# Where a mixture-of-experts result gets its weight: ScalarE after the fetch, or GpSimd before the scatter

## The chip, the core and the metric

The kernel runs on one core of a Trainium2 chip, in one launch. The metric is the device time of one execution in microseconds (us). Below, PE is TensorE, DVE is VectorE, ACT is ScalarE, POOL is GpSimd and SP is SyncE, which only issues DMAs.

## The reference

Two transformer-like layers work on x of 8 x 256 tokens of width 128. Layer 0 adds a small state-space block and a ternary feed-forward net. Layer 1 adds a "test-time training" attention (a state W per head, updated chunk by chunk) and a mixture of experts. Only the last part is touched by the change:

```python
scores = sigmoid(xf @ gate_w.T + gate_b)               # 2048 tokens, 8 experts
top_scores, top_idx = top_k(scores, 2)
top_scores = top_scores / (top_scores.sum(-1, keepdims=True) + 1e-06)
hdn = gelu(einsum('th,ehf->etf', xf, w1) + b1[:, None, :])
y = einsum('etf,efh->eth', hdn, w2) + b2[:, None, :]
routed = einsum('te,eth->th', comb, y)                 # comb: the two weights, 0 elsewhere
shared = (gelu(xf @ sw1 + sb1) @ sw2 + sb2) * 0.1
x = x + attention + routed + shared
```

So each token has two expert results, each is multiplied by one number, the token's normalised score for that choice, and both are added to the token's residual.

## The kernel before, in words

Everything is float32. Tokens lie in chunks n = 0 to 3 of 64 positions, with 4 pairs of batch rows each: a chunk is a tile of 128 partitions x 4 pairs x 128 features (`x1[n]`), and a pair is one of 16 "units" u of the attention.

**Order of the work.** After layer 0 the main loop (L1297) runs through the units. One turn works on three of them at once: unit u+1 makes its keys, unit u its normalised states, unit u-1 its gradient and its update of W, and unit u-2 its output. Between these steps `filler()` puts in steps of other work: the end of layer 0's feed-forward net, the routing (turn 5), the shared expert, and from turn 6 to turn 14 the routed expert tiles. In the loop the orders of DVE and SP are the program's own (`manual_schedule`, L1291). The orders of PE, ACT and POOL are made by a list scheduler from priorities and estimated times. For the last units, from L1413 on, the orders of PE and ACT too are written by hand; POOL's never is.

**Routing.** `norm()` (L327) makes a row of ROW = 130 numbers for each token: 128 normalised features, the token's number (column D) and the rank of its first choice's expert (column D+1). `choose(0)` and `choose(1)` (L365) take the best and second score of each token into `wgt`, and `find_slots()` (L387), in a later step, gives each of the two choices a place in an HBM array `xg_dram`, sorted by expert. `scatter()` (L254) then writes rows there with indirect DMAs from POOL, 32 in all. `weights()` (L758) normalises the scores of all tokens at turn 9 with four DVE instructions.

**Routed tiles.** 39 tiles (NJ) of 128 rows follow, three to a group (GJ). For each: SP loads the expert's weights and the rows (L815, L824), PE transposes the rows (L831), makes the hidden layer (L855), ACT applies gelu (L860), PE makes the result (L870), DVE adds the bias into `ysum` (L881). `places()` (L834) works out on DVE, with two instructions for a group, where in `y_dram` each row of the result goes; it is put off to a quiet place in DVE's order. `scatter_results()` (L885) writes the 128 rows of a tile's result there with an indirect DMA from POOL. These are queued in `ready`, and `transfers(k)` in the main loop issues up to k of them at three places of a turn.

**The turn of a transfer.** Each indirect DMA has an ordering edge to the POOL instruction last noted in `turn` (L162). It is noted by `rsqrt()` (L171), which makes an inverse deviation by a multiply-add (L174) and a power of -1/2 (L175) on POOL, and by `normalise()` (L1112, L1113), which makes the start of the gradient on POOL. So a transfer does not come ahead of the POOL work that the program has just issued.

**The end.** When all tiles are scattered, `get(8)` (L1435) fetches the results again, eight tiles (first and second choice of 4 chunks). `weigh()` (L936) multiplies each with four ACT instructions, one for a pair of batch rows, at hand-chosen places (`weigh(1)`, `weigh(1)`, `weigh(4)`, `weigh(1)`, `weigh(1)`), and `add()` (L943) adds it to `x1[n]`: three on POOL (`put(3, z.last)`, L1462) and five on DVE. Then `x1` is stored.

Of the kernel before, what the change touches and what calls it, by code (L numbers as in the profile page):

```python
# [26 lines left out]
NBP = B // 2  # L27
# [4 lines left out]
NT = NCH * NBP  # L32
# [3 lines left out]
GJ = 3  # L36
# [5 lines left out]
NXG = E * CAP + (NJ - 2 * B * S // P) * P  # L42


ROW = D + 2

SLOTS = (4, 1, 2, 0, 5, 3)
SLOTS_2 = (5, 2, 4, 5, 3, 1)
# [3 lines left out]


EARLY, ROUTE = 6, 5
NORMAL = 9
AT_SILU, AT_SILU_1, AT_XP = 7, 10, 11
FFN = ((0, 2), (1, 11), (2, 16), (3, 3), (4, 4))
SHARED = ((4, 2), (5, 6), (14, 3), (15, 3), (16, 2))
# [20 lines left out]
def tile_two_layers(ctx: ExitStack, tc: tile.TileContext, t: dict, out: bass.AP):  # L79
    nc = tc.nc  # L80

    const = ctx.enter_context(tc.tile_pool(name="const", bufs=1))
    small = ctx.enter_context(tc.tile_pool(name="small", bufs=2))
# [3 lines left out]
    side = {}  # L87
# [72 lines left out]
    turn = []  # L160

    def transfer(**what):  # L162
        ins = nc.gpsimd.indirect_dma_start(**what).ins  # L163
        tc.add_manual_dep(
            ins, turn[0].name,
            mybir.DependencyInfo(mybir.DependencyClass.NoSync, mybir.DependencyReason.DATA),
            reason="in turn",
        )
        return ins
# [10 lines left out]
    def later(f):  # L180
        pending.append(f)
# [49 lines left out]
    def empty_rows(pool):  # L231
        rows = pool.tile([P, ROW], F32, tag="empty", name="empty", bufs=1)
        nc.gpsimd.memset(rows, 0.0)
        nc.gpsimd.memset(rows[:, D : D + 1], float(2 * B * S))
        nc.gpsimd.memset(rows[:, D + 1 : ROW], -1.0)
        return rows

    slot = resident_i("slot", [P, NT, 2])
# [6 lines left out]
    wgt = resident("wgt", [P, NT, 2])  # L245
# [20 lines left out]
    def ffn_steps(n):  # L266

        s = {}
# [94 lines left out]
        mine = slice(n * NBP, (n + 1) * NBP)  # L363

        def choose(k):  # L365

            shape = [P, NBP, E]
            left = t_e(s["w"][2]) if k else s["s"]
            m = wgt[:, mine, k]
            nc.vector.tensor_reduce(m, left, AX.X, ALU.max)  # L370
            eq = t_e(s["w"][k])
            nc.vector.tensor_tensor(eq, left, m.unsqueeze(2).to_broadcast(shape), ALU.is_equal)
            nc.vector.tensor_tensor(eq, eq, rank[:, None, :].to_broadcast(shape), ALU.mult)
            mr = small.tile([P, NBP], F32, tag="tk_mr", name="tk_mr") if k else s["row"][:, :, D + 1]
            nc.vector.tensor_reduce(mr, eq, AX.X, ALU.max)
            nc.vector.tensor_tensor(eq, eq, mr.unsqueeze(2).to_broadcast(shape), ALU.is_equal)
            if k == 0:
                nc.vector.scalar_tensor_tensor(t_e(s["w"][2]), eq, -4.0, s["s"], ALU.mult, ALU.add)
            else:
                sel = s["w"][3]  # L380
                nc.vector.tensor_tensor(sel, s["w"][0], s["w"][1], ALU.add)
                s["pn"] = bank("pn")[:, : 2 * NBP * E].rearrange("p (a c) -> p a c", a=2)
                nc.tensor.matmul(s["pn"][:, 0, :], lhsT=all_ones, rhs=sel, start=True, stop=True)
                nc.tensor.matmul(s["pn"][:, 1, :], lhsT=earlier, rhs=sel, start=True, stop=True)
                later(find_slots)

        def find_slots():  # L387

# [300 lines left out]
    def routing_steps():  # L689
# [65 lines left out]
            )  # L755
            load_first_tiles()

        def weights():  # L758
            tot = small.tile([P, NT], F32, tag="tk_tot", name="tk_tot")
            nc.vector.tensor_tensor(tot, wgt[:, :, 0], wgt[:, :, 1], ALU.add)  # L760
            nc.vector.tensor_scalar(tot, tot, 1e-6, None, ALU.add)
            nc.vector.reciprocal(tot, tot)
            nc.vector.tensor_tensor(wgt, wgt, tot.unsqueeze(2).to_broadcast([P, NT, 2]), ALU.mult)

        return constants, [tiles, rows], [results], weights

    def shared_steps(n, half):

# [37 lines left out]


    known, scattered = [], []
    ew, xg, xgT, hidden, ysum, unsummed, ats = {}, {}, {}, {}, {}, [], {}

    def expert_weights(j):
        if j < NJ:
# [13 lines left out]
    def routed_tokens_T(g):  # L826
        if g < NG:
            pt = bank("pxg")[:, : GJ * P].rearrange("p (j q) -> p j q", j=GJ)
            src = xg.pop(g)
            for j in range(GJ):  # L830
                nc.tensor.transpose(pt[:, j, :], src[:, j, 0:D], ident)  # L831
            ats[g] = side["moe"].tile([P, GJ], I32, tag="ats", name="ats", bufs=3)

            def places():  # L834

                first = small.tile([P, GJ], F32, tag="first", name="first")
                nc.vector.tensor_tensor(
                    first, src[:, :, D + 1], tile_rank[:, g * GJ : (g + 1) * GJ], ALU.is_equal
                )
                nc.vector.scalar_tensor_tensor(  # L840
                    ats[g], first, -float(B * S), src[:, :, D], ALU.mult, ALU.add
                )
                known.append(g)

            quiet.append(places)
            xgT[g] = side["moe"].tile([P, GJ, P], F32, tag="xgT", name="xgT")
            nc.scalar.copy(xgT[g], pt)
# [37 lines left out]
    def scatter_results(g, i):  # L885
        assert g in known
        scattered.append(g * GJ + i)
        ins = transfer(
            out=y_dram, out_offset=bass.IndirectOffsetOnAxis(ap=ats[g][:, i : i + 1], axis=0),
            in_=ysum[g][:, i, :], in_offset=None, bounds_check=2 * B * S - 1, oob_is_err=False,  # L890
        )

        tc.declare_no_dep(ins, group="results", reason="distinct rows")
        tc.add_to_no_dep_group("results", ins)
# [23 lines left out]
    def result_steps(n, k):  # L918

        held = {}  # L920

        def fetch():

            if n == NCH - 2:
                y = wk[:, k * NBP * D : (k + 1) * NBP * D]
            elif n < NCH - 1:
                y = side["moe"].tile([P, NEW], F32, tag="ew", name="yc", bufs=4)[:, 0 : NBP * D]
            else:
                y = side["moe"].tile([P, NBP * D], F32, tag="rhid", name="yc")
            held["y"] = y.rearrange("p (b d) -> p b d", b=NBP)  # L930
            row = k * B * S + n * TB
            nc.sync.dma_start(
                out=held["y"], in_=y_dram[row : row + TB, :].rearrange("(b p) d -> p b d", p=P)
            )

        def weigh():  # L936
            for bp in range(NBP):
                nc.scalar.activation(
                    held["y"][:, bp, :], held["y"][:, bp, :], AF.Copy,
                    scale=wgt[:, n * NBP + bp, k : k + 1],  # L940
                )

        def add(behind=None):  # L943
            if behind is None:
                nc.vector.tensor_tensor(x1[n], x1[n], held["y"], ALU.add)  # L945
# [8 lines left out]
        return fetch, weigh, add  # L954


    Wst = [l1.tile([P, 2, HH, HD], F32, tag=f"W_{bp}", name=f"W_{bp}") for bp in range(NBP)]
# [318 lines left out]
    constants, to_tiles, to_loads, weights = routing_steps()  # L1276
# [7 lines left out]
    fill[NORMAL] += [weights]  # L1284
# [12 lines left out]
    for u in range(units - 1):  # L1297
# [3 lines left out]
        z, g, o = live.get(u), live.get(u - 1), live.pop(u - 2, None)  # L1301
# [74 lines left out]
            g.outputs_std()  # L1376
        transfers(2)
        for _ in range(gets.get(u, 0)):
            fetch, weigh, add = results.pop(0)
            fetch()  # L1380
            weigh()
# [4 lines left out]
    weighed, added = [], []  # L1386

    def last_filler(u, k):

# [3 lines left out]
    def get(k):  # L1393
        assert NJ - 1 in scattered and not ready
        for _ in range(min(k, len(results))):
            fetch, weigh, add = results.pop(0)
            fetch()
            weighed.append(weigh)
            added.append(add)

    def weigh(k):
        for _ in range(min(k, len(weighed))):
            weighed.pop(0)()

    def put(k, behind=None):
        for _ in range(min(k, len(added))):
# [3 lines left out]
    results = [results[k] for k in (0, 1, 2, 3, 6, 7, 4, 5)]  # L1410
# [22 lines left out]
    g.steps_of_W()  # L1433
    transfers(len(ready))
    get(8)  # L1435
    weigh(1)
    o.outputs_T()
    flush()
    g.outputs()
    z.open_queries()  # L1440
    weigh(1)
    o.open_mix()
    o.mix_heads()
    last_filler(u, len(fill[u]))
    u += 1
    z.means(first)
    g.outputs_std()
    weigh(4)
    z.gradient(first)
    last_filler(u, 2)  # L1450
    z.steps_of_W(first)
# [10 lines left out]
    put(3, z.last)  # L1462
    z.outputs(HALVES)
    z.last_std()
    weigh(1)
    last_filler(u, len(fill[u]))
    z.normalise_outputs(first)
    z.outputs_T(first)
# [2 lines left out]
    put(1)  # L1471
    g.residual()
    flush_all()
    weigh(1)
    put(2)
    z.open_mix()
    z.mix_heads(first)
# [109 lines left out]
```

## Time and profile before

| what | value |
|---|---|
| median of 4 runs | 579.21 us (573.93 to 580.35) |
| the profiled execution's own time | 574.86 us |
| its span in the profile | 573.2 us |
| granted TensorE clock over the span | 0.988 |
| PE busy | 534.1 us (93%) |
| DVE busy | 404.7 us (71%) |
| POOL busy | 296.3 us (52%) |
| ACT busy | 259.2 us (45%) |
| turns with routed tiles, about 305 to 530 us | PE has little idle time |
| last units, 530 to 573 us | PE busy 30.2 us of 43, DVE 35.5, ACT 29.2, POOL 24.5 |

The span is what the profile shows from the first to the last instruction; the time has 1.7 us more around it. A line of a timeline gives the start, the duration (of a run of equal instructions), the engine, the kernel's line, the operation, the tiles it writes and reads, how often, and in brackets the idle time of that engine just before it with what ended it.

### The profile page before, as it was taken

The page shows a single profiled execution, that of the slowest core. Times are in us where ns is not written, and L with a number is a line of the kernel's source. Part 1 is how long each engine was busy: PE and PEld are TensorE (multiplying, and loading weights), DVE is VectorE, ACT ScalarE, POOL GpSimd, SP SyncE. Part 2 cuts the span into 40 slices and gives each one's busy share as a digit, 9 for nine tenths or more (in the row PEclk, how much of TensorE's full clock was granted, in tenths as well). Part 3 has the DMA queues.
Part 4 walks back from the last instruction along what each step waited for, and adds up shares of the span by engine and source line. Part 5 has one row for each costly group of instructions (what it writes and reads, how often), then busy time and mean ns, then how long its engine had stood idle before and what let it go on. Part 6 is the DMA issues. An engine that isn't in the chain of part 4 may idle for free. (4 is left out here: it accounts for less than half of the span.)

```text
span 573.2 us, 14199 instructions
## 1 busy us (share of the span) xinstructions
PE 534.1 (93%) x5891; PEld 369.3 (64%) x5891; DVE 404.7 (71%) x649; ACT 259.2 (45%) x472; POOL 296.3 (52%) x258
## 2 busy tenths in 40 slices
PE   6999999999999999999979999999999999999695
PEld 3443655465456546476766887877787777878584
DVE  4697353457931476667979788869789777757995
ACT  4655545315430542224416363452645454453685
POOL 5216103851680156443674557565865737384861
PEclk9999999999999999999989999999999999989989
DMA  7900200000000000000153434442443433300312
GB/s 274 396 39 26 61 2 6 33 1 3 9 26 4 1 9 15 17 0 2 43 182 98 146 112 149 148 150 97 159 150 103 150 111 134 99 15 4 99 51 74
DMA packets 25200, 45.89 MB, mean 80 GB/s; under 512 B 3875, under 2 KB 16297, under 8 KB 24624
## 3 DMA queue, kind: packets, MB, share of 16 engines
q1 hardware_dynamic: 22864, 40.75, 21.6%
q0 software_dynamic: 2272, 4.24, 2.3%
q8 instruction: 46, 0.75, 0.5%
q14 instruction: 18, 0.15, 0.1%
HBM read 38.30 MB, written 7.13 MB: 79 GB/s over the span
## 5 line engine op out<-in xcount | busy, mean ns | idle before, releaser
L293 PE MATMUL pm<-g,h 128*128 128x512 f32 x256 | 113.6, 594 | 0.0
L175 POOL TENSOR_TENSOR rstd<-rs_v,neg_half 128x16 f32<-128x16 f32 x31 | 93.1, 3003 | 2.6
L293 PEld LDWEIGHTS pm<-g,h 128*128 128x128 f32 x256 | 48.2, 190 | 59.8 <-issue 57.3
L1112 POOL TENSOR_TENSOR gx<-xh,gam 128x1024 f32<-128x1024 f32 (+1 forms) x17 | 37.9, 2229 | 72.2 <-DVE er L1111 60.1
L860 ACT ACTIVATE rhid<-phd,ew 128x128 f32<-128x128 f32 x156 | 44.5, 374 | 41.1 <-issue 21.0
L297 ACT ACTIVATE g<-pm,cols 128x512 f32<-128x512 f32 x32 | 22.0, 687 | 75.5 <-PE pm L293 75.5
L174 POOL TENSOR_SCALAR rs_v<-var 128x16 f32<-128x16 f32 x31 | 7.3, 235 | 91.2 <-DVE var L1048 90.5
L163 POOL DMA_INDIRECT y_dram<-ys,ats x39 | 43.2, 1107 | 8.9 <-issue 8.5
L1048 DVE TENSOR_REDUCE var<-sq 128x16 f32<-128x1024 f32 (+1 forms) x33 | 38.9, 1180 | 9.4 <-ACT sq L1042 9.4
L855 PE MATMUL phd<-xgT,ew 128*128 128x128 f32 x312 | 43.5, 280 | 1.1 <-DMA ew<-in_moe_w 1.0
L855 PEld LDWEIGHTS phd<-xgT,ew 128*128 128x128 f32 x312 | 39.3, 191 | 7.5 <-issue 5.5
L1042 ACT ACTIVATE sq<-o 128x1024 f32<-128x1024 f32 (+1 forms) x17 | 17.1, 1010 | 54.7 <-DVE o L1031 54.7
L870 PE MATMUL pyr<-ew,rhid 128*128 128x128 f32 x312 | 41.4, 276 | 0.0
L163 POOL DMA_INDIRECT xg_dram<-xn,slot x32 | 35.9, 1121 | 8.6 <-issue 7.7
L1113 POOL TENSOR_TENSOR gx<-gx,u 128x1024 f32<-128x1024 f32 (+1 forms) x17 | 38.7, 2276 | 1.3
L870 PEld LDWEIGHTS pyr<-ew,rhid 128*128 128x128 f32 x312 | 38.0, 192 | 0.7 <-issue 0.5
L1088 DVE TENSOR_TENSOR u<-rows_b,pv 128x1024 f32<-128x1024 f32 x16 | 19.5, 1217 | 23.9 <-PE pv L976 23.9
L1260 PE MATMUL po<-wo,oT 128*128 128x128 f32 x256 | 33.1, 285 | 0.7 <-ACT oT L993 0.7
L1260 PEld LDWEIGHTS po<-wo,oT 128*128 128x128 f32 x256 | 31.9, 202 | 1.2 <-ACT oT L993 0.9
L976 PE MATMUL pk<-wk,xnT 128*128 128x512 f32 x64 | 32.2, 623 | 0.2 <-DVE o L1031 0.2
L976 PE MATMUL pv<-wv,xnT 128*128 128x512 f32 x64 | 31.4, 613 | 0.0
L1005 PE MATMUL pq<-xnT,wq 128*128 128x256 f32 x128 | 30.8, 383 | 0.7 <-DVE B L1207 0.7
(233 smaller groups left out, 1067.5 us busy)
## 6 DMA issues: line engine op xcount, KB each, us to landing
ew<-in_moe_w SPq DMA_DIRECT2D x39, 578.0 KB
xg<-xg_dram SPq DMA_DIRECT2D x39, 65.0 KB
h<-in_h SPq DMA_DIRECT2D x2, 1024.0 KB
yc<-y_dram SPq DMA_DIRECT2D x6, 256.0 KB
rows_g<-in_rows_g SPq DMA_DIRECT2D x1, 1024.0 KB
rows_b<-in_rows_b SPq DMA_DIRECT2D x1, 1024.0 KB
w<-in_w SPq DMA_DIRECT2D x3, 256.0 KB
x<-in_x SPq DMA_DIRECT2D x3, 256.0 KB
```

What stands on the lines that cost most here:

```text
L163: ins = nc.gpsimd.indirect_dma_start(**what).ins
L175: turn[:] = [nc.gpsimd.tensor_tensor(dst, v[:, :width], neg_half[:, :width], ALU.pow).ins]
L293: nc.tensor.matmul(pm, lhsT=w[:, k, m * P : (m + 1) * P], rhs=s[src][:, k, :], start=(k == 0), stop=(k == 3),)
L855: nc.tensor.matmul(ph[:, ms], lhsT=w[:, ms], rhs=xgT[j // GJ][:, j % GJ, :], start=True, stop=True)
L860: nc.scalar.activation(hid[:, m, :], ph[:, ms], AF.Gelu, bias=w[:, C_EB1 + m : C_EB1 + m + 1])
L870: nc.tensor.matmul(py, lhsT=hid[:, m, :], rhs=w[:, C_EW2 + m * D : C_EW2 + (m + 1) * D], start=(m == 0), stop=(m == 3),)
L976: nc.tensor.matmul(pp[:, j, :], lhsT=xT, rhs=w[:, j * 512 : (j + 1) * 512], start=True, stop=True)
L1005: nc.tensor.matmul(pq[:, i, :], lhsT=wq[:, (h0 + i) * P : (h0 + i + 1) * P], rhs=xnT[n][:, 2 * half : 2 * half + 2, :], start=True, stop=True,
L1048: nc.vector.tensor_reduce(v[:, heads], sq[:, heads], AX.X, ALU.add)
L1112: nc.gpsimd.tensor_tensor(g, xh, gam2[:, k], ALU.mult)
L1113: turn[:] = [nc.gpsimd.tensor_tensor(g, g, self.t[:, k], ALU.add).ins]
L1260: nc.tensor.matmul(self.po, lhsT=self.oT[:, hp, :], rhs=wo[:, hp, :], start=False, stop=(hp == HH - 1),)
```

## The change

The row of a token grows from 130 to 132 numbers. The normalisation of the scores moves from turn 9 into `choose(1)`, chunk by chunk, behind the issue of its two matmuls, and writes into the row: column D+2 gets the first weight less the second, column D+3 the second. `places()` works out, with two more DVE instructions for a group, the weight of each row's choice (`gains`): the difference times "this tile is the first choice's expert", plus the second. `scatter_results()` multiplies the tile's result in place by that number on POOL, ahead of the indirect DMA, and notes that multiply in `turn`. `weigh()` and all its calls go, so that the fetched tiles are added as they come.

```diff
-ROW = D + 2
+ROW = D + 4
...
-NORMAL = 9
...
-        nc.gpsimd.memset(rows[:, D + 1 : ROW], -1.0)
+        nc.gpsimd.memset(rows[:, D + 1 : D + 2], -1.0)
...
                 nc.tensor.matmul(s["pn"][:, 1, :], lhsT=earlier, rhs=sel, start=True, stop=True)
+                weights()
                 later(find_slots)
+
+        def weights():
+
+            w = wgt[:, mine, :]
+            tot = small.tile([P, NBP], F32, tag="tk_tot", name="tk_tot")
+            nc.vector.tensor_tensor(tot, w[:, :, 0], w[:, :, 1], ALU.add)
+            nc.vector.tensor_scalar(tot, tot, 1e-6, None, ALU.add)
+            nc.vector.reciprocal(tot, tot)
+            nc.vector.tensor_tensor(
+                s["row"][:, :, D + 2 : ROW], w, tot.unsqueeze(2).to_broadcast([P, NBP, 2]), ALU.mult
+            )
+            one, two = s["row"][:, :, D + 2], s["row"][:, :, D + 3]
+            nc.vector.tensor_tensor(one, one, two, ALU.subtract)
...
-        def weights():
-            tot = small.tile([P, NT], F32, tag="tk_tot", name="tk_tot")
-            nc.vector.tensor_tensor(tot, wgt[:, :, 0], wgt[:, :, 1], ALU.add)
-            nc.vector.tensor_scalar(tot, tot, 1e-6, None, ALU.add)
-            nc.vector.reciprocal(tot, tot)
-            nc.vector.tensor_tensor(wgt, wgt, tot.unsqueeze(2).to_broadcast([P, NT, 2]), ALU.mult)
...
+            gains[g] = side["moe"].tile([P, GJ], F32, tag="gains", name="gains", bufs=3)
...
                 nc.vector.scalar_tensor_tensor(
                     ats[g], first, -float(B * S), src[:, :, D], ALU.mult, ALU.add
                 )
+                nc.vector.tensor_tensor(first, first, src[:, :, D + 2], ALU.mult)
+                nc.vector.tensor_tensor(gains[g], first, src[:, :, D + 3], ALU.add)
...
         scattered.append(g * GJ + i)
+        y = ysum[g][:, i, :]
+        turn[:] = [nc.gpsimd.tensor_scalar(y, y, gains[g][:, i : i + 1], None, ALU.mult).ins]
         ins = transfer(
...
-        def weigh():
-            for bp in range(NBP):
-                nc.scalar.activation(
-                    held["y"][:, bp, :], held["y"][:, bp, :], AF.Copy,
-                    scale=wgt[:, n * NBP + bp, k : k + 1],
-                )
-
...
     get(8)
-    weigh(1)
     o.outputs_T()
     flush()
     g.outputs()
     z.open_queries()
-    weigh(1)
...
     g.outputs_std()
-    weigh(4)
     z.gradient(first)
...
     z.last_std()
-    weigh(1)
...
     flush_all()
-    weigh(1)
     put(2)
```

More of the change, by code (lines that the diff above doesn't have):

```diff
@@ L756, in results @@
             load_first_tiles()
-        def weights():
-            tot = small.tile([P, NT], F32, tag="tk_tot", name="tk_tot")
-            nc.vector.tensor_tensor(tot, wgt[:, :, 0], wgt[:, :, 1], ALU.add)
-            nc.vector.tensor_scalar(tot, tot, 1e-6, None, ALU.add)
-            nc.vector.reciprocal(tot, tot)
-            nc.vector.tensor_tensor(wgt, wgt, tot.unsqueeze(2).to_broadcast([P, NT, 2]), ALU.mult)
-        return constants, [tiles, rows], [results], weights
+        return constants, [tiles, rows], [results]
     def shared_steps(n, half):
@@ L808, in tile_two_layers @@
     known, scattered = [], []
-    ew, xg, xgT, hidden, ysum, unsummed, ats = {}, {}, {}, {}, {}, [], {}
+    ew, xg, xgT, hidden, ysum, unsummed, ats, gains = {}, {}, {}, {}, {}, [], {}, {}
     def expert_weights(j):
@@ L952, in add @@
                 )
-        return fetch, weigh, add
+        return fetch, add
     Wst = [l1.tile([P, 2, HH, HD], F32, tag=f"W_{bp}", name=f"W_{bp}") for bp in range(NBP)]
@@ L1275, in tile_two_layers @@
         fill[turn_u] += [steps.pop(0) for _ in range(k)]
-    constants, to_tiles, to_loads, weights = routing_steps()
+    constants, to_tiles, to_loads = routing_steps()
     fill[ROUTE - 1] += [open_moe]
@@ L1283, in tile_two_layers @@
     fill[ROUTE] += to_loads
-    fill[NORMAL] += [weights]
     routed = [lambda j=j: routed_step(j) for j in range(NJ + 1)]
@@ L1378, in tile_two_layers @@
         for _ in range(gets.get(u, 0)):
-            fetch, weigh, add = results.pop(0)
+            fetch, add = results.pop(0)
             fetch()
-            weigh()
             fetched.append(add)
@@ L1385, in tile_two_layers @@
     first, second = HALVES
-    weighed, added = [], []
+    added = []
     def last_filler(u, k):
@@ L1395, in get @@
         for _ in range(min(k, len(results))):
-            fetch, weigh, add = results.pop(0)
+            fetch, add = results.pop(0)
             fetch()
-            weighed.append(weigh)
             added.append(add)
-    def weigh(k):
-        for _ in range(min(k, len(weighed))):
-            weighed.pop(0)()
     def put(k, behind=None):
```

## The prediction, made before the changed kernel ran

> **What bounds the kernel now.** I read the page's busy times first, then busy time by stretch, then the groups by shape for the lines the change touches, then the timelines of the last 45 us and of one routed turn. The page and the stretches:
>
> ```profile
> PE 534.1 (93%) x5891; PEld 369.3 (64%) x5891; DVE 404.7 (71%) x649; ACT 259.2 (45%) x472; POOL 296.3 (52%) x258
> ```
> ```profile
> 285.00:530.00 245.00, 231.34 (x3551) 187.97 (x3549) 195.14 (x259) 111.23 (x240) 151.14 (x98) 0.99 0.37 118
> 530.00:573.00 43.00, 30.16 (x438) 26.02 (x428) 35.50 (x51) 29.24 (x84) 24.48 (x16) 0.92 0.25 75
> ```
>
> In the columns of the second fence (length, PE, weight loads, DVE, ACT, POOL) PE is busy 231 of the 245 us from 285 to 530: it sets the pace there, and POOL and DVE have about 94 and 50 us free. In the last 43 us no engine is full: there a chain through DVE, PE, ACT and POOL decides. What the change removes and the only sort of POOL work near to what it adds:
>
> ```profile
> L938 ACT ACTIVATE yc<-yc,wgt 128x128 f32<-128x128 f32 x24 | 7.2, 389 | 0.0
> L938 ACT ACTIVATE wk<-wk,wgt 128x128 f32<-128x128 f32 x8 | 2.5, 390 | 0.0
> ```
> ```profile
> L163 POOL DMA_INDIRECT y_dram<-ys,ats x39 | 43.2, 1107 | 8.9 <-issue 8.5
> L174 POOL TENSOR_SCALAR rs_v<-var 128x16 f32<-128x16 f32 x31 | 7.3, 235 | 91.2 <-DVE var L1048 90.5 <-issue 0.2
> L619 POOL COPY bpad<-headT 128x1024 f32<-128x1024 f32 x1 | 1.5, 1494 | 0.0
> ```
>
> The timeline of the end, ACT, then POOL, then DVE:
>
> ```profile
> 547.40 5.95 ACT L938 ACTIVATE yc<-yc,wgt 128x128 f32<-128x128 f32 x20
> 553.83 1.64 ACT L784 ACTIVATE hid<-pm,shared_w 128x256 f32<-128x256 f32 x4 [0.48 <-PE pm L778]
> ...
> 563.87 1.26 ACT L938 ACTIVATE wk<-wk,wgt 128x128 f32<-128x128 f32 x4
> 565.68 1.13 ACT L993 COPY oT<-poT 128x512 f32<-128x512 f32 x2 [0.55 <-PE poT L989]
> 566.71 1.28 ACT L938 ACTIVATE wk<-wk,wgt 128x128 f32<-128x128 f32 x4
> ```
> ```profile
> 531.68 2.91 POOL L175 TENSOR_TENSOR rstd<-rs_v,neg_half 128x16 f32<-128x16 f32 x1
> 534.77 1.06 POOL L163 DMA_INDIRECT y_dram<-ys,ats  x1 [0.18 <-issue]
> 536.13 0.97 POOL L163 DMA_INDIRECT y_dram<-ys,ats  x1 [0.30 <-issue]
> 537.17 0.67 POOL L174 TENSOR_SCALAR rs_v<-var 128x16 f32<-128x16 f32 x1
> 537.93 3.91 POOL L175 TENSOR_TENSOR rstd<-rs_v,neg_half 128x16 f32<-128x16 f32 x1
> ```
> ```profile
> 541.87 0.69 DVE L1107 TENSOR_TENSOR xh<-xh,rstd 128x512 f32<-128x512 f32 x1 [0.24 <-POOL rstd L175]
> ...
> 566.41 1.42 DVE L945 TENSOR_TENSOR x<-x,yc 128x512 f32<-128x512 f32 x2
> 567.75 1.47 DVE L945 TENSOR_TENSOR x<-x,wk 128x512 f32<-128x512 f32 x2
> ```
>
> The reader is to see that after each block of weighting ACT still waits for PE (0.48 and 0.55 us): ACT was early, not late. And that the last two scatters stand ahead of a POOL power that DVE waits for.
>
> **The weighting goes from ACT.** 32 instructions of 0.39 us, 12.4 us with their gaps, all between 543.0 and 568.0. The first block (543.01 to 544.28) is followed by a copy that waits 1.26 us for PE; the five blocks from 547.40 by 0.48 us of waiting for PE; the one at 563.87 by 0.55 us; the last ends at 567.99, before DVE's last add, which starts at 568.52 directly behind the add ahead of it. The consumers do not wait either: POOL's three adds start at 557.83 and are tied to DVE's last gradient step at 557.7, and DVE's five adds from 565.50 run back to back, in an order that does not change. I take a gain of 0. The bound below is 0.5 us, in case the order of the last microseconds loosens a little.
>
> **The multiply on POOL.** 39 of 128x128 with a number per partition; no row of the trace is such an instruction. The nearest in kind is L174, 0.20 us undisturbed for 16 columns, and the single-input copy L619 takes 1.49 us for 1024. The line between them gives 0.20 + 112 x 1.28 ns = 0.34 us; I take that. Below, 0.20 us (a POOL memset of 128x128 is 0.20); above, 1.0 us, since L174 took 0.67 us at 537.17 beside a busy DVE, over three times its 0.20. 39 x 0.34 = 13.3 us.
>
> Where does it lie? 37 of the 39 scatters are issued from 324 to 530 us. There POOL waits 48.9 us for DVE's er ahead of L1112 and 18.4 us for the variance. The cover, turn by turn, is the time from the end of the power (L175) to the DVE instruction that reads it. For example the power at 389.38 ends at 392.32 and is read at 396.77: 4.45 us, the least of the normalising ones in the routed turns from 310 to 516; the output's power ahead of it ends at 385.51 and is read at 390.05, 4.54 us. The product of L1113 has at least 4.23 us until L1117 reads it. A turn has four to five scatters, two or three of them together: three multiplies are 1.0 us. Cost 0 there; if the cover were gone, 13 us.
>
> The two scatters at 534.77 and 536.13 have no cover. DVE had been done with its gradient at 541.64 and waits for the power that ends at 541.84. Two multiplies, 0.68 us, and two gaps of 0.08 us as between L174 and L175, push it: **+0.84 us**, which goes through to the end, since DVE, PE and ACT follow in one chain (PE's L1020 at 546.13 waits for DVE's L1031). By the bounds, 0.5 to 2.2 us.
>
> The multiply waits for the bias add and for `gains`, both on DVE. Behind it stand the powers, whose variance DVE makes later than that bias add; the wait holds nobody up that would not wait anyhow. The eight fetches by SP wait for the last scatter and start 0.8 us later; they start at 538.34 and are first read at 557.8, so this is hidden.
>
> The Trainium skill speaks against such a place: GPSIMD Engine Reference, section 4.1, Engine selection, gives elementwise work to VectorE, with single-input instructions at about its rate, and section 1 lets GpSimd share VectorE's SBUF interfaces, with contention for instructions of two SBUF inputs. The row first: POOL's power took 2.91 us at 531.68 and 3.91 at 537.93, while DVE's tensor_tensor ran in both, so the trace shows some such loss but not always. By the first rule alone the sum is as above (DVE's 128x128 tensor_scalar L216 takes 0.34 us); by the second at its worst the two end multiplies are 1.0 us each and the sum is 1.3 us higher.
>
> **More work on DVE.** (a) 26 more instructions in `places()`, each 0.165 us (L837 161 ns, L840 164 ns), 0.33 us a group. I went through the 13 groups in DVE's timeline. Nine meet DVE idle time before PE needs DVE (for instance 1.60 us at 480.97 after the group at 479.02, 3.42 at 464.60 after that at 459.45), one has 0.39 us of slack ahead of PE's L1187 at 369.69. Three do not: at 444.37 W ends at 447.47 and PE loads it at 447.53 (0.33), at 396.30 with 0.13 us of slack (0.20), at 494.00 PE waits 0.4 us for the gradient (0.33). **+0.86 us**; bounds 0 and 4.3.
> (b) 20 instructions for the weights, 0.17 to 0.25 us each, 0.97 us a chunk. They stand where DVE goes on to wait for PE's `pn`: 2.96 us in chunk 0, 0.56 in chunk 1, 0 in chunk 2 (DVE next idles 2.78 us at 215.29), 0.82 in chunk 3. Chunks 1 and 2 end up to 0.97 us late in a stretch in which PE has other work (busy 40.0 of 40 us from 140 to 180); chunk 3 is 0.15 us late and feeds the scatters behind which DVE waits 1.24 us for POOL. **+0.15 us**; bounds 0 and 3.9.
> (c) Four instructions at 386.99 go, 0.82 us up to the next start at 387.80. DVE runs without a pause from there to its L1241, for which PE waits 0.79 us at 391.42: **-0.79 us**; bounds -0.8 and 0.
>
> **Wider rows.** 528 bytes for 520 in 32 scatters and 39 loads of 65 KB: 1.5% more, 39 KB, at the 118 GB/s of that stretch 0.3 us spread over 200. PE's waits for DMA there are 1.0 us in all. Cost 0, at most 0.3.
>
> **The sum.** 0 + 0.84 + 0.86 + 0.15 - 0.79 + 0 = +1.06 us on 574.86 us, the profiled execution's own time (span 573.2 and 1.66 around it): 575.9. That execution lies near the fastest run; the median is 579.21, so I forecast 579.21 + 1.1 = **580.3 us**. 1% of it, 5.8 us, is about what a measurement of this kernel can tell from no change.
>
> **The rivals.**
> 1. *POOL's order.* Before, a scatter was tied behind the power or product just issued. Now it is tied only behind its multiply, and the multiply is tied to nothing, so the scheduler may put pairs ahead of a power. A pair costs 0.34 + 0.08 + 1.01 + 0.30 = 1.73 us. Two fit in the least cover of 4.45 us; with three it decides: 5.2 - 4.45 = 0.75 us late in each of nine routed turns, 6.7 us, and 0.84 at the end: 586.8. For it: nothing else orders the multiply. Against: POOL idles 67 us at such places, so early pairs mostly fall into them.
> 2. *DVE becomes the bound* and all its new work counts: 4.3 + 3.9 - 0.8 + 0.84 = 8.2 us, 587.4. For it: DVE is 80% busy from 285 to 530. Against: its waits for PE in the same stretch.
> 3. *Faster.* PE, ACT and POOL are reordered in the loop when estimated times change. PE idles 13.7 us from 285 to 530; were half of it closed, -6.9 + 1.1: 573.4. For it: scatters freed of their turn can move into POOL's 48.9 us of idle time, so that the power at 508.61 is not 3.3 us behind its variance. Against: its reader has 7.2 us left as it is.
> That ACT's work was the bound after all is excluded by the waits above.
>
> **How the numbers follow.** Forecast 0.55, rival 1 0.19, rival 2 0.14, rival 3 0.12. The likeliest case's own range is 577 to 584. Its 0.55 lies within 1% but for 0.02 on each side; of the slower rivals 0.31 of 0.33 is over 1% (the multiply's upper bounds add to them); of rival 3 0.11 is over 1%, the rest within. So faster 0.13, within 0.54, slower 0.33. The range must reach into rivals on both sides: 574 (rival 3's better half left out) to 588 (both slower rivals' centres).
>
> **What would show it.** Right: no L938 on ACT and no earlier DVE adds from about 566; 39 POOL TENSOR_SCALAR of about 0.34 us; PE as busy as now from 285 to 530; DVE's wait at the first half of L1107 in the last unit about 1.1 us instead of 0.24. Wrong: scatters ahead of L174 in the routed turns with DVE waiting for rstd at L1107 or L1241 (rival 1); new PE waits for gx or W (rival 2); multiplies near 1 us; less PE idle time (rival 3).

## The result, and the profile after

The changed kernel took 578.88 us (median of 44 runs, 574.28 to 584.09), the kernel before 575.96 us (median of 70 runs, 572.20 to 580.35). The ratio is 1.0041, with a 95% interval of 1.0025 to 1.0057: slower by 2.4 us (1.4 to 3.3), so well within 1%, on the side that was forecast. The ratio goes by the fast executions alone, without the four slowest of after, so it is not the quotient of the two medians. The profiled execution of after took 577.86 us (span 576.2), that of before 574.86 (span 573.2). Most lines of after lie 6 to 14 further down: the multiply is L900, the bias add L892 (before L881), the gradient's start on POOL L1118 and L1119 (L1112, L1113), `places()` L846 to L853 (L837, L840).

The page's busy times after, then busy time by stretch (length, PE, weight loads, DVE, ACT, POOL, each with its number of instructions, then the granted clock):

```profile
PE 533.9 (93%) x5891; PEld 369.5 (64%) x5891; DVE 423.3 (73%) x691; ACT 249.9 (43%) x440; POOL 345.4 (60%) x297
```
```profile
285.00:530.00 245.00, 230.49 (x3530) 187.57 (x3532) 210.65 (x281) 111.21 (x240) 195.62 (x136) 0.98 0.37 118
530.00:576.00 46.00, 31.02 (x462) 26.73 (x454) 35.95 (x51) 20.01 (x52) 27.48 (x17) 0.90 0.23 70
```

PE has as much work as before and is as busy in the routed turns (230.49 us of 245, before 231.34). ACT lost 9.3 us and 32 instructions. POOL gained 49.1 us and DVE 18.6 us. The forecast's terms were 13.3 us for POOL's multiplies and 26 x 0.165 + 16 x about 0.2 = 7.5 us for DVE, so both engines took far more than the new instructions should need. The groups by shape show where it is (busy us, mean ns, idle time before and its releasers), POOL's first, then those of DVE:

```profile
L900 POOL TENSOR_SCALAR ys<-ys,gains 128x128 f32<-128x128 f32 x39 | 35.9, 920 | 18.5 <-DVE ys L892 12.8 <-DVE first L846 4.9
L163 POOL DMA_INDIRECT y_dram<-ys,ats x39 | 47.1, 1208 | 10.7 <-POOL ys L900 9.9 <-POOL gx L1119 0.5 <-DVE ys L892 0.3
L174 POOL TENSOR_SCALAR rs_v<-var 128x16 f32<-128x16 f32 x31 | 11.1, 358 | 76.7 <-DVE var L1054 75.1
```
```profile
L846 DVE TENSOR_TENSOR first<-xg,tile_rank 128x3 f32<-128x3 f32 x13 | 6.9, 528 | 0.0
L852 DVE TENSOR_TENSOR first<-first,xg 128x3 f32<-128x3 f32 x13 | 6.3, 483 | 0.4
L849 DVE SCALAR_TENSOR_TENSOR ats<-first,xg 128x3 int32<-128x3 f32 x13 | 5.1, 389 | 0.5
L853 DVE TENSOR_TENSOR gains<-first,xg 128x3 f32<-128x3 f32 x13 | 2.4, 185 | 0.4
```

On the mean the multiply is 0.92 us and not 0.34, the scatter 1.21 instead of 1.11, the multiply-add ahead of a power 0.36 instead of 0.24. The mean of the multiply hides two sorts: in the timeline 26 of the 39 take 0.60 to 0.62 us, the other 13 take 1.24 to 1.65. On DVE even the two steps of `places()` that were there before (0.15 to 0.17 us in the timeline of before) now take 0.53 and 0.39 us. And ahead of the multiplies POOL waits 12.8 us for DVE's bias add.

The end in the timeline of after: POOL, then DVE, then ACT (start, duration, the instruction, and in brackets the engine's idle time before it with what ended it):

```profile
526.87 2.37 POOL L1118 TENSOR_TENSOR gx<-xh,gam 128x1024 f32<-128x1024 f32 x1 [6.37 <-DVE er L1117]
529.24 0.61 POOL L900 TENSOR_SCALAR ys<-ys,gains 128x128 f32<-128x128 f32 x1
529.83 2.34 POOL L1119 TENSOR_TENSOR gx<-gx,u 128x1024 f32<-128x1024 f32 x1
532.34 1.09 POOL L163 DMA_INDIRECT y_dram<-ys,ats  x1 [0.18 <-POOL gx L1119]
533.49 1.54 POOL L900 TENSOR_SCALAR ys<-ys,gains 128x128 f32<-128x128 f32 x1
535.30 1.02 POOL L163 DMA_INDIRECT y_dram<-ys,ats  x1 [0.28 <-POOL ys L900]
536.40 0.20 POOL L174 TENSOR_SCALAR rs_v<-var 128x16 f32<-128x16 f32 x1
536.68 2.93 POOL L175 TENSOR_TENSOR rstd<-rs_v,neg_half 128x16 f32<-128x16 f32 x1
539.71 1.17 POOL L174 TENSOR_SCALAR rs_v<-var 128x16 f32<-128x16 f32 x1
540.96 3.94 POOL L175 TENSOR_TENSOR rstd<-rs_v,neg_half 128x16 f32<-128x16 f32 x1
```
```profile
544.93 0.69 DVE L1113 TENSOR_TENSOR xh<-xh,rstd 128x512 f32<-128x512 f32 x1 [2.79 <-POOL rstd L175]
...
570.79 1.41 DVE L951 TENSOR_TENSOR x<-x,wk 128x512 f32<-128x512 f32 x2
```
```profile
556.87 1.64 ACT L791 ACTIVATE hid<-pm,shared_w 128x256 f32<-128x256 f32 x4 [6.64 <-PE pm L785]
...
568.73 1.14 ACT L999 COPY oT<-poT 128x512 f32<-128x512 f32 x2 [1.71 <-PE poT L995]
```

Between the last full gradient start and the last power's end POOL now needs 18.03 us (526.87 to 544.90) instead of 15.33 (526.51 to 541.84), and DVE's wait for that power grew from 0.24 to 2.79 us. One multiply stands between the two steps of the gradient's start, both scatters stand ahead of both powers (before, they stood between them), the second multiply takes 1.54 us beside a busy DVE, and L174 takes 1.17 us where it took 0.67. The wait carries through: DVE's last adds start 3.04 us later (570.79, before 567.75). ACT's waits for PE (6.64 us at 556.87, before 0.48) grew by what the weighting used to fill, so its removal opened nothing there.

Against that, the last full gradient start was only 0.36 us later than before. In this pair of executions 2.6 of the 3.0 us of difference arise behind it, at the end. That suggested theory T, which the first experiments were made to test: only the end pays, and the routed turns hide their multiplies. Its rival was that POOL's order in the routed turns costs too and the pair of profiles hides it. A pair can: each profile has a few 3.4 us pieces at half the granted clock, worth up to 1.7 us each (half of 3.4, an estimate); before 530 us there are two in before and three in after.

That order had changed. Here is one routed turn in the timeline of POOL, first the gradient's start before, then the turn after, then DVE's `er` after:

```profile
422.06 2.35 POOL L1112 TENSOR_TENSOR gx<-xh,gam 128x1024 f32<-128x1024 f32 x1 [4.33 <-DVE er L1111]
```
```profile
419.58 1.24 POOL L900 TENSOR_SCALAR ys<-ys,gains 128x128 f32<-128x128 f32 x1
421.12 1.51 POOL L163 DMA_INDIRECT y_dram<-ys,ats  x1 [0.29 <-POOL ys L900]
424.49 1.50 POOL L900 TENSOR_SCALAR ys<-ys,gains 128x128 f32<-128x128 f32 x1 [1.87 <-DVE ys L892]
426.27 1.02 POOL L163 DMA_INDIRECT y_dram<-ys,ats  x1 [0.28 <-POOL ys L900]
427.32 2.38 POOL L1118 TENSOR_TENSOR gx<-xh,gam 128x1024 f32<-128x1024 f32 x1
```
```profile
425.43 0.17 DVE L1117 TENSOR_TENSOR er<-rstd,eta 128x16 f32<-128x16 f32 x1
```

A multiply waits 1.87 us for its bias add, and behind it in POOL's queue stands the gradient's start. Its last input, DVE's `er`, was ready at 425.60, so it begins 1.72 us late; before, it began 0.06 to 0.07 us after `er` in every routed turn. In the eight routed units from the second on it is 2.88, 3.60, 3.60, 3.60, 1.72, 1.73, 1.73 and 1.73 us late. The time from the end of the product (L1119) to DVE's first read of it shrank from 4.23 to 7.60 us to 0.03 to 3.95 us.

### The profile page after: what moved, and what is told of

Same layout as the page of the kernel before. It is cut to its first block, busy times and chain, and to the rows that moved or that the text cites. A ratio compares the mean times of both kernels' runs of the same rounds, so it can differ in the third digit from the quotient of the medians.

```text
span 576.2 us, 14276 instructions
## 1 busy us (share of the span) xinstructions
PE 533.9 (93%) x5891; PEld 369.5 (64%) x5891; DVE 423.3 (73%) x691; ACT 249.9 (43%) x440; POOL 345.4 (60%) x297
## 3 DMA queue, kind: packets, MB, share of 16 engines
q1 hardware_dynamic: 22864, 40.81, 21.6%
## 4 chain that ended last, share of the span: by engine, by line
PE 59%; DVE 16%; POOL 13%; issue 6%; ACT 3%; another core or an unknown queue 1%; DMA 1%; SPq 0%; DVEq 0%; POOLq 0%; ACTq 0%
PE pm L293 19%; PE pq L1011 4%; PE pv L982 4%; POOL y_dram L163 4%; PE pk L982 3%; POOL rstd L175 3%; PE po L1266 3%; PE po L304 2%; POOL ys L900 2%; PE pb L1200 2%; PE phd L866 2%; PE pz L1026 2%; PE pyr L881 2%; POOL gx L1118 2%; PE py L800 1%
## 5 line engine op out<-in xcount | busy, mean ns | idle before, releaser
L175 POOL TENSOR_TENSOR rstd<-rs_v,neg_half 128x16 f32<-128x16 f32 x31 | 97.0, 3128 | 2.6
L174 POOL TENSOR_SCALAR rs_v<-var 128x16 f32<-128x16 f32 x31 | 11.1, 358 | 76.7 <-DVE var L1054 75.1
L163 POOL DMA_INDIRECT y_dram<-ys,ats x39 | 47.1, 1208 | 10.7 <-POOL ys L900 9.9
L1118 POOL TENSOR_TENSOR gx<-xh,gam 128x1024 f32<-128x1024 f32 (+1 forms) x17 | 38.1, 2241 | 21.3 <-DVE er L1117 11.3
L900 POOL TENSOR_SCALAR ys<-ys,gains 128x128 f32<-128x128 f32 x39 | 35.9, 920 | 18.5 <-DVE ys L892 12.8
L163 POOL DMA_INDIRECT xg_dram<-xn,slot x32 | 37.6, 1174 | 8.6 <-issue 7.5
L881 PE MATMUL pyr<-ew,rhid 128*128 128x128 f32 x312 | 41.4, 276 | 0.0
L1119 POOL TENSOR_TENSOR gx<-gx,u 128x1024 f32<-128x1024 f32 (+1 forms) x17 | 38.7, 2274 | 1.1
L881 PEld LDWEIGHTS pyr<-ew,rhid 128*128 128x128 f32 x312 | 38.0, 192 | 0.1
L982 PE MATMUL pv<-wv,xnT 128*128 128x512 f32 x64 | 33.1, 642 | 0.0
```

Of the source, the lines that this page charges most:

```text
L175: turn[:] = [nc.gpsimd.tensor_tensor(dst, v[:, :width], neg_half[:, :width], ALU.pow).ins]
L881: nc.tensor.matmul(py, lhsT=hid[:, m, :], rhs=w[:, C_EW2 + m * D : C_EW2 + (m + 1) * D], start=(m == 0), stop=(m == 3),)
L900: turn[:] = [nc.gpsimd.tensor_scalar(y, y, gains[g][:, i : i + 1], None, ALU.mult).ins]
L982: nc.tensor.matmul(pp[:, j, :], lhsT=xT, rhs=w[:, j * 512 : (j + 1) * 512], start=True, stop=True)
L1118: nc.gpsimd.tensor_tensor(g, xh, gam2[:, k], ALU.mult)
L1119: turn[:] = [nc.gpsimd.tensor_tensor(g, g, self.t[:, k], ALU.add).ins]
```

## Experiments

Ratios are to the kernel before on the same chip, with 95% intervals. Three chips were used for the experiments, and on the first every kernel ran faster (before: 558.38, 578.39 and 575.57 us), so medians are compared only within one. The kernel after itself was not run on the first.

In the traces PE and DVE execute their instructions in the same order in after and in all its versions below (in no_multiply two of PE's 5891 are exchanged), and ACT does too in in_turn and no_multiply. So in_turn differs from after in POOL's order alone, and no version owes its time to a new order of PE or DVE.

### First chip: the end, the order, the multiply and the weighting apart

**tail_on_act.** The last two tiles are weighted on ScalarE, all others as in after:

```diff
-        turn[:] = [nc.gpsimd.tensor_scalar(y, y, gains[g][:, i : i + 1], None, ALU.mult).ins]
+        if g * GJ + i >= NJ - 2:
+            nc.scalar.activation(y, y, AF.Copy, scale=gains[g][:, i : i + 1])
+        else:
+            turn[:] = [nc.gpsimd.tensor_scalar(y, y, gains[g][:, i : i + 1], None, ALU.mult).ins]
```

> The changed kernel, but the last two routed tiles are weighted by ScalarE instead of GpSimd; the other 37 multiplies stay on GpSimd. Theory T (the end pays: the changed kernel's 2.4 us over the kernel before come from the two multiplies ahead of the last units' power, for which VectorE waits 2.79 us instead of 0.24): the ratio to the kernel before falls from 1.004 to 0.998 to 1.001, and VectorE's wait at the first half of its normalising step of the last unit is under 0.6 us. Rival R (the routed turns pay: 37 multiplies of 0.6 to 1.65 us and VectorE steps held up to 2.8 us beside them): the ratio stays at 1.003 to 1.005.

Measured: 565.23 us, ratio 1.0124 (1.0099 to 1.0149). The wait at the end is cured, as the timeline of DVE shows (each edit moves the lines: L1113 of after is L1116 here, L1112 in no_multiply and L1119 in in_turn):

```profile
532.35 0.69 DVE L1116 TENSOR_TENSOR xh<-xh,rstd 128x512 f32<-128x512 f32 x1 [0.24 <-POOL rstd L175]
```

Yet the kernel is 6.9 us slower than before. So theory T falls on this chip: with nothing lost at the end, the turns before it lose more than the whole change does elsewhere.

**no_multiply.** The multiply line is left out (the routed results are added unweighted); all else, the wider rows and DVE's new steps too, is as in after.

> The changed kernel without any multiply, so that the routed results are added unweighted; the wider rows, VectorE's added work and the removal of ScalarE's weighting stay. Theory T: the same as with the last two on ScalarE, ratio 0.997 to 1.001, since the other 37 multiplies are hidden. Rival R: clearly under the one with the last two on ScalarE, by 2 us or more (ratio 0.994 to 0.997 there, or 1.000 here with 1.004 there). If VectorE's added work were the cause, the ratio stays at 1.004.

Measured: 559.26 us, ratio 1.0016 (0.9999 to 1.0033). Nearly all of what tail_on_act loses belongs to the multiplies and where they stand: 1.0124 less 1.0016 is 6.0 us. The waits of DVE and PE from 285 to 515 us (in all, how often, the longest) show a smaller part of it; first tail_on_act, then no_multiply:

```profile
DVE xh L1116 <- POOL rstd L175: 2.6, 2, 1.4
...
DVE o L1250 <- POOL rstd L175: 0.3, 1, 0.3
...
DVE s L1126 <- POOL gx L1122: 0.2, 1, 0.2
```
```profile
DVE xh L1112 <- POOL rstd L175: 1.2, 1, 1.2
```

DVE waits 3.1 us for POOL instead of 1.2 (and PE 3.8 us instead of 0.9 for ACT's copy). A larger part lies in DVE instructions that take longer. The 52 steps of `places()` take 20.4 us in tail_on_act and 9.2 in no_multiply, for the same work. Both kernels start the same group of them at 344.76 us; POOL, then DVE of tail_on_act, then DVE of no_multiply:

```profile
344.46 2.38 POOL L1121 TENSOR_TENSOR gx<-xh,gam 128x1024 f32<-128x1024 f32 x1
346.92 2.36 POOL L1122 TENSOR_TENSOR gx<-gx,u 128x1024 f32<-128x1024 f32 x1
```
```profile
344.76 2.11 DVE L846 TENSOR_TENSOR first<-xg,tile_rank 128x3 f32<-128x3 f32 x1
...
347.10 2.20 DVE L852 TENSOR_TENSOR first<-first,xg 128x3 f32<-128x3 f32 x1
```
```profile
344.76 0.20 DVE L846 TENSOR_TENSOR first<-xg,tile_rank 128x3 f32<-128x3 f32 x1
...
345.19 0.16 DVE L852 TENSOR_TENSOR first<-first,xg 128x3 f32<-128x3 f32 x1
```

In no_multiply the gradient's start had ended at 344.61, ahead of the group. In tail_on_act it starts late, stands beside the group, and two steps of DVE last until its two steps end. Instruction by instruction, DVE of tail_on_act falls behind by 10.7 us at seven such steps and by 1.9 us at waits for POOL's power; it gets about half of this back where DVE of no_multiply waits for PE and ACT, and 4.9 us are left between the two profiled spans.

**in_turn.** The multiply gets the ordering edge that the scatter had, so that it can't come ahead of the power or gradient just issued:

```diff
-        turn[:] = [nc.gpsimd.tensor_scalar(y, y, gains[g][:, i : i + 1], None, ALU.mult).ins]
+        ins = nc.gpsimd.tensor_scalar(y, y, gains[g][:, i : i + 1], None, ALU.mult).ins
+        tc.add_manual_dep(ins, turn[0].name, ..., reason="in turn")
+        turn[:] = [ins]
```

> The changed kernel, but each multiply is tied behind the GpSimd instruction last noted, as the scatters were before, so that no pair goes ahead of a power or of the gradient's start. Theory T: no better, ratio 1.003 to 1.006, because both multiplies of the end still stand ahead of the last power. The rival of the order (pairs moved ahead cost the time): ratio 0.999 to 1.001, with the covers of the powers in the routed turns back at 4 us and more.

Measured: 562.00 us, ratio 1.0054 (1.0037 to 1.0071), by the ratios 3.9 us less than tail_on_act although the end is not cured. POOL's group in in_turn, a routed turn in its timeline, then DVE at the end:

```profile
L900 POOL TENSOR_SCALAR ys<-ys,gains 128x128 f32<-128x128 f32 x39 | 26.8, 691 | 0.1
```
```profile
430.51 0.77 POOL L900 TENSOR_SCALAR ys<-ys,gains 128x128 f32<-128x128 f32 x1
431.57 1.51 POOL L163 DMA_INDIRECT y_dram<-ys,ats  x1 [0.29 <-POOL ys L900]
436.80 2.37 POOL L1124 TENSOR_TENSOR gx<-xh,gam 128x1024 f32<-128x1024 f32 x1 [3.72 <-DVE er L1123]
```
```profile
528.09 0.69 DVE L1119 TENSOR_TENSOR xh<-xh,rstd 128x512 f32<-128x512 f32 x1 [1.50 <-POOL rstd L175]
```

Now POOL waits for DVE's `er` with nothing in front, the multiplies wait for no bias add (0.1 us of idle time instead of 18.5), and they are shorter, because they meet other instructions of DVE. The 52 steps of `places()` take 11.2 us. Of its 3.0 us over before, 1.26 are the end's wait (1.50 less 0.24). The ratio is where T had it and not where the rival of the order had it (0.999 to 1.001); but T can't be the reason, since tail_on_act, without the end's loss, stands above it.

**before_no_weigh.** The kernel before with an empty `weigh()` (results added unweighted):

```diff
         def weigh():
-            for bp in range(NBP):
...
+            pass
```

> The kernel before without ScalarE's weighting behind the fetch, so that the routed results are added unweighted; nothing else is changed. The forecast's 0 for this step: ratio 0.999 to 1.001. The rival (ScalarE's 12.4 us lay partly on the path): ratio 0.990 to 0.998, and the changed kernel's added work then costs more than 2.4 us.

Measured: 557.64 us, ratio 0.9982 (0.9966 to 0.9998). The weighting on ACT was worth about 1.0 us (0.1 to 1.9). Between this and no_multiply lie 0.0034, about 1.9 us with some 1.3 us either way: DVE's 42 more instructions and the wider rows, with what of the planned orders they move (PE's in the routed stretch at one place, a step of a routed tile that comes earlier, from 385 to 404 us).

### Second chip: both cures, and the weighting early on ScalarE

before_again and after_again are the two kernels unchanged; in_turn_tail_on_act has both edits from above; all_on_act has all 39 multiplies on ScalarE, ahead of the scatters:

```diff
-        turn[:] = [nc.gpsimd.tensor_scalar(y, y, gains[g][:, i : i + 1], None, ALU.mult).ins]
+        nc.scalar.activation(y, y, AF.Copy, scale=gains[g][:, i : i + 1])
```

> The kernel before once more, for its profile on the same chip as the runs beside it: ratio 1.000, routed turns as short as in the kernel before without weighting (21.6 to 26.3 us from one start of the gradient to the next), and the last step of 16.2 us.

> The changed kernel on the same chip as the runs beside it. New theory T2 (the loose order costs in the routed turns what the tail does not explain, since the version with the last two on ScalarE was at 1.0124 though its last wait was gone): ratio 1.014 to 1.019 on a chip on which the kernel before takes about 558 us, routed turns 1 to 2 us longer than those of the kernel before, and about 2.7 us more in the last units. Theory T (only the end pays): 1.004 to 1.006.

> The changed kernel with both cures: multiplies tied behind the GpSimd instruction last noted, and the last two on ScalarE. T2: the version in turn was at 1.0054, its last step 1.3 us (0.0023) longer than before; so 1.002 to 1.004 here, near the version without a multiply (1.0016). Theory T: no better than in turn alone.

> The changed kernel with all 39 results weighted by ScalarE ahead of the scatter, so that GpSimd's order is as before and only the place of the multiply differs. T2 (GpSimd's queue is the cause, not the early weighting): 1.000 to 1.004, for 39 x 0.39 us on an engine that is 45% busy. If any multiply ahead of the scatter cost the time: 1.010 and more.

| run | median us | ratio to before | interval |
|---|---|---|---|
| before_again | 579.58 | 1.0010 | 0.9986 to 1.0034 |
| after_again | 581.29 | 1.0055 | 1.0027 to 1.0083 |
| in_turn_tail_on_act | 577.78 | 0.9996 | 0.9969 to 1.0022 |
| all_on_act | 581.13 | 1.0039 | 1.0013 to 1.0065 |

before_again shows that two runs of one kernel agree within the interval. after_again repeats the result. It does not show the larger loss that tail_on_act had on the first chip: on this chip the kernel before takes 578 us, near to its first measurement, and its routed turns are as long as there (24.1 to 27.5 us) and not the 21.6 to 26.3 that had been expected. So T2's forecast for a chip of 558 us was not tested. The kernel with both cures stands where before stands, lower than T2 (1.002 to 1.004) and T (no better than in_turn) had it.

all_on_act costs about as much as after, at the upper end of what T2 had, so taking POOL out of it is not enough. In its timeline ACT waits for bias adds in the middle of the routed stretch:

```profile
424.04 1.16 ACT L871 ACTIVATE rhid<-phd,ew 128x128 f32<-128x128 f32 x4
425.59 0.40 ACT L900 ACTIVATE ys<-ys,gains 128x128 f32<-128x128 f32 x1 [0.40 <-DVE ys L892]
430.98 0.40 ACT L900 ACTIVATE ys<-ys,gains 128x128 f32<-128x128 f32 x1 [4.99 <-DVE ys L892]
```

Its 39 weightings (0.405 us each) have 49.8 us of idle time for bias adds ahead of them (24 waits), and three gelus behind such weightings stood idle 5.8 us for them in the trace. How much of that reaches PE was not taken apart.

### Third chip: the two cures alone and together

The four kernels are after, in_turn, tail_on_act and the one with both, beside before on one chip.

> The changed kernel once more, beside the three below on one chip, so that the two suspected causes can be taken apart. Two causes (T3): GpSimd's loose order in the routed turns, and the two multiplies ahead of the end's power. Ratio 1.004 to 1.007 where the kernel before takes about 577 us, 1.014 to 1.019 where it takes about 558.

> Only the order cured: each multiply tied behind the GpSimd instruction last noted. T3: what is left is the end, 1.3 us (0.002): 1.001 to 1.004. If only the end pays (T), no better than 1.003; if only the order pays, 0.999 to 1.001.

> Only the end cured: the last two tiles weighted on ScalarE, the other multiplies free in GpSimd's order. T3: what is left is the order: 1.001 to 1.004 on a chip of about 577 us, 1.010 to 1.014 on one of about 558 us, on which the kernel before has shorter routed turns and so more to lose. If only the end pays (T): 0.999 to 1.001 on any chip.

> Both cured. T3 and T: 0.998 to 1.003, and lower than each cure alone by what the other is worth.

| run | median us | ratio to before | interval |
|---|---|---|---|
| four_after | 579.03 | 1.0038 | 1.0008 to 1.0068 |
| four_in_turn | 577.04 | 0.9991 | 0.9957 to 1.0025 |
| four_tail_on_act | 577.05 | 1.0006 | 0.9971 to 1.0041 |
| four_both | 575.96 | 0.9982 | 0.9949 to 1.0014 |

Each cure by itself brings the kernel back to within what can be told from before, and both together do too. The end's cure is worth 0.0032, about 1.8 us, the order's 0.0047, about 2.7 us (half of the end's wait among it), and both 0.0056, about 3.2 us; each has some 2.6 us either way, so how the loss of 2.2 us divides between end and order is open on this chip. For each cure alone the third theory, T3, had expected 1.001 to 1.004; tail_on_act came out where T had it and in_turn where "only the order" had it, and the intervals cover all of these. Their waits at the first half of the last unit are the same as elsewhere, in DVE's timeline of four_after, then of four_both:

```profile
545.88 0.69 DVE L1113 TENSOR_TENSOR xh<-xh,rstd 128x512 f32<-128x512 f32 x1 [2.79 <-POOL rstd L175]
```
```profile
545.27 0.69 DVE L1122 TENSOR_TENSOR xh<-xh,rstd 128x512 f32<-128x512 f32 x1 [0.24 <-POOL rstd L175]
```

No version that weights the results is faster than the kernel before by more than its interval.

## Why the prediction was right, and where its steps were not

The time (578.88 for 580.3) and the side of the difference fell where they were forecast, but this is in part luck. The difference is +2.4 us (1.4 to 3.3), and the forecast's +1.1 lies below that interval; the median of before that it was added to, 579.21 of four runs, lies 3.2 us above the one of 70 runs; and the sum has errors of both signs in it.

**ACT's weighting, forecast 0.** The waits read off the profile were real, and ACT waits by so much more now. before_no_weigh has a gain of about 1.0 us (0.1 to 1.9): more than 0, in the direction that the prediction named, while the bound of 0.5 lies inside the interval. The 12.4 us that it gave the weighting are the durations added up; back to back they overlap (20 in 5.95 us), and the four blocks take 9.8 us.

**The multiply, forecast 0.34 us.** It took 0.92 us on the mean, inside the bounds (0.20 to 1.0): 0.60 to 0.62 undisturbed and 1.2 to 1.7 beside some instructions of DVE. The line drawn through L174 and the copy L619 was 0.27 us short even undisturbed. The upper bound, from the slowed L174, was passed by 13 of the 39: a stretch by two to nearly three times came to every third multiply, and the mean stayed under the bound.

**The end, forecast +0.84 us with a bound of 2.2.** It is +2.55 us (2.79 less 0.24), above the bound, in after and again in after_again and four_after. This is the term that went wrong most, and the reason is in POOL's timeline: the two multiplies are 0.61 + 1.54 = 2.15 us instead of 0.68, and L174 is 0.50 us longer. That the order there changes as well, the prediction had not taken into its sum. Where it said that this wait goes through to the end it was right: the last adds are 3.04 us later, and the cure of the end takes the wait back to 0.24.

**"The wait holds nobody up that would not wait anyhow."** This step failed. It took POOL's order as it was, with the powers behind the multiply. The planner put multiplies also ahead of the gradient's start L1118, where a bias add that is not ready holds up a product that is: 1.7 to 3.6 us in each of eight units. That is the order of rival 1, which had 0.19. Its price, 6.7 us of DVE's waits for POOL in the turns, was not paid in that form: most of the delay fell into the cover (4.23 us at the least before, 0.03 at the least now), and from 285 to 515 us DVE waits for POOL 1.7 us after and 1.2 before. What the late product costs is what it then stands beside, DVE's steps of `places()` (next paragraph). On the first chip 6.0 us lie between tail_on_act and no_multiply, and 3.9 us come back with the order restored. On the chips with 576 to 578 us DVE's waits for PE took it in, by these rows: from 285 to 515 us they are 36.2 us in before and 24.0 in after. On the first chip there is less of them to begin with, 24.3 us in before_no_weigh, and the routed turns take 21.6 to 26.3 us there and 23.9 to 27.5 on the chip of the first profile. So less is left to cover a delay; that this is the reason was not tested.

**More work on DVE, forecast +0.86 + 0.15 - 0.79 = +0.22 us.** On the first chip about 1.9 us (some 1.3 either way), within the bounds but above the value taken; what it is made of was not taken apart. The instructions cost what their like did when POOL stands still: 0.15 to 0.18 us. What was missed is that the ones of `places()` get stuck behind POOL once the multiplies have put its product beside them; in no_multiply only two of the 52 do. In DVE's timeline of after, and POOL's for the same moment:

```profile
378.05 0.15 DVE L846 TENSOR_TENSOR first<-xg,tile_rank 128x3 f32<-128x3 f32 x1
378.24 2.81 DVE L849 SCALAR_TENSOR_TENSOR ats<-first,xg 128x3 int32<-128x3 f32 x1
381.08 0.16 DVE L852 TENSOR_TENSOR first<-first,xg 128x3 f32<-128x3 f32 x1
```
```profile
378.07 0.61 POOL L900 TENSOR_SCALAR ys<-ys,gains 128x128 f32<-128x128 f32 x1
378.67 2.35 POOL L1119 TENSOR_TENSOR gx<-gx,u 128x1024 f32<-128x1024 f32 x1
```

A step of 0.17 us lasts until the product on POOL is done (381.05 and 381.02). In the kernel before this did not happen: the 13 steps of each kind took 0.161 and 0.164 us on the mean. So the step that failed is the fixed price of 0.165 us: 52 steps at that price are 8.6 us, and in after they take 20.7 (6.9 + 6.3 + 5.1 + 2.4).

**Rival 2** (DVE the bound, 8.2 us) did not come: PE is as busy as before. **Rival 3** (faster) did not come either.

The rule on contention that the prediction had weighed can now be set beside numbers. The Trainium skill, GPSIMD Engine Reference, section 1, Specifications, has GpSimd share its SBUF interfaces with VectorE, with contention when an instruction of VectorE has two SBUF inputs. The runs agree: all 13 stretched multiplies of after began beside such an instruction, and the price was the whole overlap and not a share of it. The prediction's worst case, 1.0 us for each multiply at the end, was still below the 1.54 us of the second one.

With the measured terms the sum is -1.0 + 2.55 + 1.9 = about +3.5 us, just above the total's interval (1.4 to 3.3); the terms come from different chips. So the total came out near although the end cost three times its forecast: what ACT gave stood against it, and DVE's waits for PE took in what POOL's order did to the turns. The sum had the first at 0 and nothing for the second.

## What to carry to other kernels

Work given to an engine because it is idle half of the time is hidden only where its instructions can't stand in front of those that others wait for: look at what follows it in that queue, and give it an ordering edge of its own if the neighbour had one. Ask also what the delayed work will then stand beside: here it held up short steps of another engine. Price a short GpSimd instruction by what it takes beside a busy VectorE, and count what it does to VectorE's own short instructions. Keep new work off the last chain, where there is no cover: two of 39 multiplies made a wait of 2.55 us there.

## What the runs showed of the hardware that was not expected

- POOL's multiply, multiply-add and product and DVE's instructions with two SBUF inputs waited for one another by whole instructions. The multiply took 0.60 to 0.62 us while DVE reduced or added out of PSUM, and up to 1.67 us when DVE ran a tensor_tensor of two SBUF inputs, ending 0.4 to 0.5 us after that one; L174 took 0.20 or 1.17 us in the same way. The other way round a DVE step of 128x3 took 2.81 us instead of 0.17 behind POOL's product. POOL's power and indirect DMA did not hold such steps up: in after four of them took 0.16 to 0.17 us each at 463.16, in the middle of a power of 2.93 us, and 0.15 to 0.16 at 364.56 beside a scatter.
- An undisturbed tensor_scalar of 128x128 on POOL with a number per partition takes 0.61 us; ACT's weighting of the same shape takes 0.39 us on the mean in the kernel before and 0.41 in all_on_act.
- The same kernel took 558 us on one chip and 576 to 578 us on two others. The granted clock over the span (0.992 to 0.997 there, 0.98 to 0.99 in most runs elsewhere) is about 0.01 apart, or 6 us. A part of the rest lies in PE: up to the gradient's start at 224 us the two are level (223.85 in before, 224.06 in before_no_weigh), and behind it a block of 64 small matmuls (L1020) that takes 1.16 us in before_no_weigh takes up to 3.6 us in before, with gaps of 0.2 to 0.4 us in it that nothing in the profile ends. From 224 us on such gaps of PE add up to 4.7 us in before and 5.7 in before_again, and there are none in the four kernels profiled on the first chip. What makes them stays open.
